# A cross-attention block on one core: its table of order and its table of places written anew

## The chip, the cores and the metric

The kernel runs on one core of a Trainium2 chip. The metric is the device time of one execution in microseconds (us). The kernel before was run three times: 654.65, 653.41 and 654.18, a median of 654.18. One more execution was taken with the hardware profiler; all durations of single instructions come from it.

## The reference

A transformer block with cross-attention in fp32: x and the context are 8 x 256 x 512 (batches, tokens, channels), 16 heads of 32 channels.

```python
residual = hidden_states
x = layer_norm(hidden_states, ln1_w, ln1_b)
q = (x @ q_w + q_b).reshape(B, LQ, H, HD).transpose(0, 2, 1, 3)
k = (encoder_hidden_states @ k_w + k_b).reshape(B, LK, H, HD).transpose(0, 2, 1, 3)
v = (encoder_hidden_states @ v_w + v_b).reshape(B, LK, H, HD).transpose(0, 2, 1, 3)
scores = jnp.einsum('bhqd,bhkd->bhqk', q, k) * scale
scores = jnp.where(mask, scores, mask_value)
attn = jax.nn.softmax(scores, axis=-1)
out = jnp.einsum('bhqk,bhkd->bhqd', attn, v).transpose(0, 2, 1, 3).reshape(B, LQ, D)
hidden = out @ cproj_w + cproj_b + residual
y = layer_norm(hidden, ln2_w, ln2_b)
y = jax.nn.gelu(y @ fc_w + fc_b, approximate=True)
return hidden + y @ proj_w + proj_b
```

fc_w is 512 x 2048, proj_w 2048 x 512.

## The kernel before, in words

**Work.** The eight batches go in two groups, 0 and 1, of four. The large products (q, k, v, the output projection o, the two of the MLP, fc and pd) are made by Strassen's method as Winograd arranged it: seven half-size products P1 to P7 in place of eight, added up in three PSUM banks X, Y and W and then evicted in pieces (t1, t2, t3, c11, c12, c21, c22; the function `quad`, L852). A tile named k1_0_W is bank W of the keys' product for group 1, half 0. An eviction that only copies is L601, one that adds a bias L606 on ScalarE and L608 on VectorE; one that adds to what is there already is L625. The sums of operands that the method needs are L623 and L625 on VectorE or GpSimd: c..t of the context, x..t and y..t of the normalized tokens, a..t of the attention, and those of the MLP's weights (fw, pw), which go to DRAM and come back as fl and pl.

**Attention.** It is done in units, named by group, quarter of the heads and batch within the group (s132: group 1, heads 12 to 15, batch 2). A unit has scores s (TensorE, four heads at once, in four PSUM banks of its own), eight evictions ev into pr (ScalarE, L614, with the mask), two maxima mx (VectorE, L1033), three copies mc (ScalarE, L1039), a fold and a transpose (VectorE, L1040 and L1042), a trip through DRAM that spreads the maximum over the partitions (md, mm), two subtractions less (VectorE L1053, or GpSimd L1057 in two pieces each), two exponentials (ScalarE, L1060), in some units halved sums ss, the product av with its row sums (TensorE, one bank), the inverse r of the sums (VectorE, L1083, L1085, L1086) and the scaling att (VectorE, L625), after which the bank of av is free. Layer norm takes BN_STATS (L802) and BN_AGGR (L804) on VectorE for each tile.

**Order.** No scheduler runs when the kernel is built. The functions only record operations, each with the engines that can do it. `Order.run` (L94) then reads two tables. PROGRAM lists all 2999 operations in one planned order; a letter behind a colon is the engine (P TensorE, V VectorE, A ScalarE, G GpSimd, S SyncE), and without a letter it is the operation's first one. Each engine gets its instructions in this order and runs them strictly in it. All DMAs are issued from SyncE's queue, in the same order. PLACES gives 1304 buffers their slot: one of eight PSUM banks for X, Y, W, s and av, or a slot in SBUF. An operation whose buffer lies in a slot that another held waits until the other's last reader is done:

```python
for word in PROGRAM.split():
    name, _, e = word.partition(":")
    o = ops.pop(name)
    o.eng = letters[e] if e else o.alts[0][0]
    order.append(o)
...
where = dict(p.split("=") for p in PLACES.split())
for o in order:
    for b in o.bufs:
        if b.slot is None and b.name in where:
            b.slot = int(where[b.name])
```

Of the kernel before, what the change touches and what calls it, by code (L numbers as in the profile page):

```python
# [127 lines left out]
rows5 c0_30:A eps_x0_1 v0_0_P2 rows4 rows6 fw0_10_0 c0t4:V v0_1_t2:V v0_0_t3:A pow_x0_1 nb_x0_1 norm_x0_11:A mk kw11
rows8 v0_1_P2 fw0_00_1 v0_0_P3 kws3:V mk~1 fw0i4_3:G fw0_10_1 cols fw0_00_0 xt0_5 v0_1_P5 fw0i4_2:V xt0_6 fw0i4_4:V
kws1:V kws2:V cols~1 k0_0_t1:A k0_1_t1:V xt0_0 k0_1_P6 v0_0_c11 xt0_7 fw0_01_0 fw0s3:V v0_1_t3:A xt0_1 fw0s1:G  # L130
fw0i5_1:G v0_1_c11 stats_x0_31 k0_0_P7 stats_x0_21 k0_1_t2:A fw0i5_2:G kw01 xt0_4 fw0_01_1 fcd0_5_False fcd0_7_False
stats_x0_00 fw0i5_3:V fw0i1_1:V fcd0_4_True fw0i7_1:G fw0i1_3:V k0_0_P6 qw00 k0_0_t2:A aggr_x0_00 fw0i7_2:V fw0i7_4:V
v0_1_P3 fw1_01_0 k0_1_P2 k0_0_P5 fw0i1_2:V fw0s2:V norm_x0_10:A aggr_x0_21 fw1_00_0 qw11 aggr_x0_31 fw0i5_4:V qw01
fw0i1_4:V k0_1_P5 vd0_0_11 stats_x0_01 aggr_x0_01 fw1_01_1 eps_x0_0 v0_1_c12:A kws4:G fw0i7_3:V v0_0_c12:A stats_x0_20
aggr_x0_20 pow_x0_0 stats_x0_30 aggr_x0_30 nb_x0_0 k0_0_t3:V k0_0_P2 fw0i2_1:G norm_x0_00:A eps_x0_2 fw1_00_1
fw0i2_2:V pow_x0_2 k0_1_P7 eps_x0_3 nb_x0_2 norm_x0_20:A fcd0_5_True norm_x0_01:V k0_1_t3:A norm_x0_21:A fcd0_7_True
cb1_11 fcd0_1_True pow_x0_3 k0_1_c11 nb_x0_3 fw0i6_3:G turn_x0_10 fw0i6_1:V fw0i6_2:G k0_0_P3 x0_10:A xt1_3 fw0i6_4:G
# [15 lines left out]
ev022_20 mx002_0 v0_1_c22 c1t1:G ev022_30 ev022_21 ev022_31 mx022_1 md020 ev022_10 less000_0:G less000_1:G v0_0_c22
cb1_20 mc002_3 ev022_01 mc002_1 mc002_2 fold002 fcd1_6_False v0_1_P4 ev022_11 mm020 q0_1_c21 v0_1_c21 mf002 ev022_00
v0_0_P4 mx022_0 exp000_0 norm_x1_11:A s010 mc022_3 mc022_1 k1_0_P1 exp000_1 cb1_33 cb1_30 cb1_32 mc022_2 ss000_0:G
cT1_20 cb1_31 v0_0_c21 ev010_30 ev010_11 md002 less020_1:V ev010_00 ev010_21 fold022 ev010_01 ev010_31 fcd1_5_True
ev010_20 ss000_1:G k1_1_P1 kd0_1_22 cT1_21 mf022 ev010_10 less020_0:V av000 s030 exp020_0 cT1_31 cT1_30 norm_x1_10:A
fcd1_6_True md022 k1_1_t1:A xt1_7 ev030_21 ev030_01 mx010_1 ev030_30 xd1_3 r000 att000 k1_0_P2 mx010_0 ev030_00
k1_0_t1:A c1t2:G k1_1_P6 exp020_1 ev030_31 ev030_20 ev030_11 k1_0_c11 mc010_1 mc010_2 mc010_3 c1t3:G kd0_1_12
ss020_0:V ev030_10 kd0_1_21 mm022 xt1_4 k1_0_P6 k1_0_t2:A ss020_1:V xt1_0 av020 stats_x1_31 mx030_1 mx030_0 aggr_x1_31  # L160
fold010 k1_1_t2:A s012 xt1_6 stats_x1_30 ev012_21 fcd1_7_True mc030_2 mc030_1 ev012_31 xt1_1 r020 k1_1_P5 stats_x1_01
att020 mf010 k1_0_P5 mm002 mc030_3 aggr_x1_30 xd1_2 kd0_0_22 k1_0_P7 less022_1:G exp022_1 md010 less022_0:G
stats_x1_00 ev012_20 exp022_0 ss022_0:V ev012_01 vd0_0_21 ku011 less002_1:V ev012_00 k1_0_t3:A mm010 less002_0:V
ev012_30 ev012_11 ev012_10 aggr_x1_01 k1_1_t3:A fold030 vd0_0_12 ss022_1:G av022 c1t4:G exp002_0 s032 vu010 xt1_5
vu030 ev032_30 ev032_11 mf030 aggr_x1_00 k1_0_c22 mx012_1 vd0_1_11 k1_1_P3 ev032_10 ev032_20 ss002_0:G mx012_0 k1_0_P3
ku001 ev032_01 ev032_31 eps_x1_3 eps_x1_0 ev032_00 less010_1:V exp002_1 k1_1_P7 ss002_1:G k1_0_P4 ev032_21 mx032_1
exp010_1 k1_0_c12:A mx032_0 vd0_0_22 stats_x1_20 av002 mc032_2 md030 mc032_3 ku021 mc032_1 k1_0_c21 r022 fold032
# [5 lines left out]
norm_x1_21:A exp030_0 mx001_0 v1_1_t1:A mc001_3 ev021_31 v1_0_t1:V v1_0_P2 v1_0_P6 att010 xd1_1 v1_1_P6 less032_0:V
xd1_7 xd1_4 ev021_20 xd1_5 v1_0_c11 mc001_2 exp030_1 s003 ss030_0:G ev021_21 mc001_1 exp032_1 ev021_30 fold001
exp032_0 mf001 mx021_0 ss032_1:V mm012 v1_0_t2:A ev003_30 v1_1_t2:V md001 ev003_01 ev003_00 ss030_1:G ev003_21 av030
ss032_0:G av032 mx021_1 mc021_3 r030 mc021_1 xb1_11 mc021_2 xb1_01 less012_0:G ev003_31 fold021 ev003_10 mf021
less012_1:V xb1_13 mm001 r032 ev003_11 ev003_20 mx003_0 ku013 exp012_0 exp012_1 v1_0_P5 v1_0_t3:A s023 md021 ev023_00
# [282 lines left out]
ps_o11=0 ot1=28 ps_o01=4 ps_o10=7  # L460
# [1053 lines left out]
```

## Time and profile before

| | |
|---|---|
| median of three runs | 654.18 us |
| the profiled execution's span, first to last instruction | 652.0 us |
| TensorE busy, share of the span | 99% |
| VectorE | 89% |
| GpSimd | 61% |
| ScalarE | 53% |
| granted clock of TensorE | 1.00 in all stages |

The span leaves out what lies ahead of the first and behind the last instruction. In the profile PE is TensorE, DVE VectorE, ACT ScalarE, POOL GpSimd, SP SyncE; L625 is line 625 of the kernel. "h<-fc_X" is a tile written from a tile read, without the numbers in the names. A group's row ends with its count, its busy time, the mean of one in ns, and the idle time ahead of it with what ended it. The attention of group 0 and the keys and values of group 1 take the time up to about 143 us, the attention of group 1 and the output projection of group 0 that up to about 288, the MLP the rest.

### The profile page before, as it was taken

The numbers are of one execution on the slowest core, as the hardware profiler recorded it, in microseconds if no ns is written. First come the engines' busy times: TensorE is split into PE (matmuls) and PEld (weight loads), VectorE is DVE, ScalarE is ACT, GpSimd is POOL, SyncE is SP. The second block draws the span as 40 slices with busy tenths as digits, with TensorE's granted clock in tenths as the row PEclk, the third lists the DMA queues.
The fourth block names the chain that finished last, engine by engine and source line by source line (L and its number), as shares of the span: only waits on it lengthen the run. The fifth ranks groups of instructions, "written<-read, shape, count | busy, mean of one in ns | idle before, by whom it ended". The sixth has DMA issues, their size and how long they took to land.

```text
span 652.0 us, 11225 instructions
## 1 busy us (share of the span) xinstructions
PE 644.3 (99%) x3793; PEld 487.7 (75%) x3793; DVE 583.2 (89%) x985; ACT 346.1 (53%) x709; POOL 395.9 (61%) x351
## 2 busy tenths in 40 slices
...
GB/s 268 306 328 324 239 251 284 226 204 152 217 224 151 130 168 232 260 267 250 257 214 250 225 272 232 293 314 170 160 222 197 215 198 204 158 190 227 173 138 97
DMA packets 206713, 144.83 MB, mean 222 GB/s; under 512 B 117136, under 2 KB 167104, under 8 KB 206656
## 3 DMA queue, kind: packets, MB, share of 16 engines
...
## 4 chain that ended last, share of the span: by engine, by line
PE 90%; DVE 4%; ACT 2%; issue 1%; DMA 1%; POOL 1%; DVEq 0%
PE pd_X L634 15%; PE fc_X L634 15%; PE fc_W L634 7%; PE pd_W L634 7%; PE av L634 6%; PE q_X L634 4%; PE v_X L634 4%; PE fc_Y L634 4%; PE k_X L634 4%; PE pd_Y L634 4%; PE s L634 4%; PE o_X L634 2%; PE v_W L634 2%; PE k_W L634 2%; PE o_W L634 2%; DVE mx L1033 2%
## 5 line engine op out<-in xcount | busy, mean ns | idle before, releaser
L614 ACT ACTIVATE pr<-s,cols 128x256 f32<-128x256 f32 x256 | 102.9, 485 | 10.7 <-PE s L634 8.2
L1057 POOL TENSOR_TENSOR pr<-pr,mm 128x512 f32<-128x512 f32 x70 | 90.2, 1318 | 7.2 <-DMA xt<-in_x_dram 5.0
L1237 ACT ACTIVATE h<-h,cols 128x256 f32<-128x256 f32 x128 | 55.2, 499 | 61.2 <-DVE h L625 45.2
L1033 DVE TRANSPOSE_TENSOR_REDUCE mx<-pr 128x32 f32<-128x1024 f32 x64 | 76.9, 1216 | 1.5 <-ACT pr L614 1.3
L1060 ACT ACTIVATE pr<-pr 128x1024 f32<-128x1024 f32 x64 | 66.5, 1061 | 12.1 <-POOL pr L1057 9.0
L625 DVE TENSOR_TENSOR h<-fc_X,h 128x512 f32<-128x512 f32 x80 | 52.4, 675 | 5.5 <-PE fc_X L634 4.7
L625 POOL TENSOR_TENSOR ss<-pr 128x512 f32<-128x512 f32 x24 | 31.5, 1325 | 14.2 <-ACT pr L1060 11.8
L625 DVE TENSOR_TENSOR h<-fc_W,h 128x512 f32<-128x512 f32 x48 | 32.0, 677 | 5.0 <-PE fc_W L634 4.4
L1053 DVE TENSOR_TENSOR pr<-pr,mm 128x1024 f32<-128x1024 f32 x29 | 35.2, 1229 | 0.0
L1039 ACT COPY mx<-mx 32x64 f32<-32x64 f32 x96 | 23.2, 243 | 15.9 <-DVE mx L1033 14.7
L623 POOL TENSOR_TENSOR z1t<-h,z1t 128x512 f32<-128x512 f32 x6 | 8.0, 1360 | 26.1 <-PE pd_Y L634 12.3
L625 POOL TENSOR_TENSOR tq<-tq,rq 128x512 f32<-128x512 f32 x8 | 10.1, 1272 | 21.7 <-DMA rq<-hd 15.4
L634 PE MATMUL pd_X<-z0i,pl 128*128 128x256 f32 x96 | 22.5, 379 | 0.0
L634 PE MATMUL fc_W<-y1i,fl 128*128 128x256 f32 x84 | 20.7, 379 | 0.0
L625 DVE TENSOR_TENSOR h<-fc_Y,h 128x512 f32<-128x512 f32 x24 | 15.9, 672 | 5.3 <-PE fc_Y L634 5.3
L634 PE MATMUL pd_W<-z1i,pl 128*128 128x256 f32 x88 | 20.6, 379 | 0.0
L1040 DVE TENSOR_REDUCE mx<-mx 32x32 f32<-32x256 f32 x32 | 18.4, 578 | 2.2 <-ACT mx L1039 2.0
L634 PEld LDWEIGHTS pd_X<-z0i,pl 128*128 128x128 f32 x96 | 18.2, 190 | 2.5
L811 POOL TENSOR_TENSOR rs_y<-rs_y,neg_half 128x2 f32<-128x2 f32 x8 | 10.2, 1289 | 15.3 <-DMA pl<-prd 7.7
L634 PE MATMUL pd_X<-h,pl 128*128 128x256 f32 x80 | 18.9, 379 | 0.0
L601 ACT COPY h<-fc_X 128x512 f32<-128x512 f32 x16 | 9.0, 594 | 18.5 <-PE fc_X L634 15.6
L625 DVE TENSOR_TENSOR po<-pd_X,po 128x256 f32<-128x256 f32 x24 | 9.9, 414 | 9.6 <-PE pd_X L634 9.4
...
## 6 DMA issues: line engine op xcount, KB each, us to landing
...
```

The costliest lines, as they stand in the source:

```text
L601: (nc.scalar.copy if e == "ACT" else nc.vector.tensor_copy)(to(), of_())
L614: lambda e: nc.scalar.activation(to(), of_(), AF.Identity, bias=bias(), scale=1.0))
L625: E[e].tensor_tensor(to(), in0(), in1(), op)
L634: nc.tensor.matmul(o(), l(), r(), start=first, stop=True, skip_group_check=True)
L811: lambda e, rs=rs: nc.gpsimd.tensor_tensor(tile_of(rs)[:, 2:4], tile_of(rs)[:, 0:2], neg_half[:, 0:2], ALU.pow), lock=True)
L1033: T.op(f"mx{u}_{h}", [("DVE", 1.126)], [(pr[h], None)], [(mx, [h])], lambda e, h=h: nc.vector.tensor_reduce(tile_of(mx)[:, 0:64].rearrange ...
L1039: lambda e, a=a: nc.scalar.copy(tile_of(mx)[0:32, 64 * a : 64 + 64 * a], tile_of(mx)[32 * a : 32 * a + 32, 0:64]))
L1040: T.op(f"fold{u}", [("DVE", 0.38)], [(mx, [0, 1, 2, 3, 4])], [(mx, [5])], lambda e: nc.vector.tensor_reduce(tile_of(mx)[0:32, 256:288], ti ...
L1053: nc.vector.tensor_tensor(p_, p_, m_[:, None, :].to_broadcast([P, 2, 512]), ALU.subtract)
L1057: E[e].tensor_tensor(p_, p_, m_, ALU.subtract)
L1060: lambda e, h=h: nc.scalar.activation(tile_of(pr[h]), tile_of(pr[h]), AF.Exp), table="exp")
L1237: lambda e, f=f, b=b, c=c: nc.scalar.activation(at(h[f][b], c), at(h[f][b], c), AF.Gelu_apprx_tanh, bias=col(c_fcb + f * 4 + c), scale=1.0 ...
```

## The change

Only the two tables change; not a line of code does. Both have the same 2999 words and the same 1304 buffers. 153 words change their engine: 64 from VectorE to GpSimd, 48 from GpSimd to VectorE, 23 from ScalarE to VectorE, 18 from VectorE to ScalarE. 972 buffers change their slot. On TensorE most operations stay within four positions of where they stood; the largest moves are in the second MLP product of group 1.

One line of PROGRAM before and the one that holds the same eviction after, and lines of PLACES:

```diff
-mx013_1 mx013_0 q1_1_t1:A av003 mx031_0 q1_0_t1:A x1_30:A r001 ev033_11 ev033_21 mc013_3 mc013_2 mc031_2 q1_0_P6
+mc031_2 mc031_1 q1_1_t1:V r003 q1_0_P6 pw0_00_01 hid0_2 vu013 pw0_00_11 q1_0_t2:V fold031 att003 mf031 mc013_3 mc013_2
-mm010=4 ss010=4 av020=3 r020=1 rc020=4 att0_10=88 vu030=10 s030_0=3 s030_1=5 s030_2=6 s030_3=4 pr030_0=8 pr030_1=10
+mm010=4 ss010=70 av020=5 r020=5 rc020=9 att0_10=88 vu030=1 s030_0=5 s030_1=4 s030_2=0 s030_3=6 pr030_0=8 pr030_1=10
-rc122=1 att1_11=48 s132_0=1 s132_1=0 s132_2=5 s132_3=7 pr132_0=4 pr132_1=66 mx132=2 mm132=80 av110=1 r110=3 rc110=3
+mx112=0 mm112=54 av122=7 r122=1 rc122=6 att1_11=48 s132_0=7 s132_1=5 s132_2=3 s132_3=0 pr132_0=66 pr132_1=4 mx132=1
```

Bank 3, that of k1_0_W in both tables, is held by av020 ahead of it before, and by av000, one unit earlier, after (`av000=0` has become `av000=3`). Bank 7 is that of o0_0_W in both; the scores' buffer that holds it last is s132_3 before and s132_0 after.

The first place is on VectorE, in the attention of group 0. Before, att0_10 (the scaling of unit 020) stands behind the statistics (BN_STATS) of tiles x1_3 and x1_0:

```order
L802 BN_STATS st_x1_3_1092<-k1_1_11_1025 128x6
L1033 TENSOR_REDUCE mx030_1094<-pr030_1_1028 128x2x16
L1033 TENSOR_REDUCE mx030_1094<-pr030_0_1030 128x2x16
L804 BN_AGGR mv_x1_3_1097<-st_x1_3_1092 128x2
L1040 TENSOR_REDUCE mx010_1032<-mx010_1032 32x32
L802 BN_STATS st_x1_3_1092<-xt1_0_1077 128x6
L1083 TENSOR_REDUCE rc020_1122<-av020_1079 128x8
L1085 RECIPROCAL rc020_1122<-rc020_1122 128x8
L1086 STREAM_TRANSPOSE r020_1125<-rc020_1122 128x256
L802 BN_STATS st_x1_0_1129<-vw11_255 128x6
L625 TENSOR_TENSOR att0_10_1131<-av020_1079,r020_1125 128x256
L1042 STREAM_TRANSPOSE mx010_1032<-mx010_1032 32x32
```

After, in the same place (att0_00 and att0_10 are the scalings of units 000 and 020):

```order
L802 BN_STATS st_x1_0_1086<-xt1_0_1029 128x6
L1033 TENSOR_REDUCE mx030_1065<-pr030_1_1049 128x2x16
L625 TENSOR_TENSOR att0_00_1100<-av000_971,r000_1022 128x256
L1083 TENSOR_REDUCE rc020_1102<-av020_1071 128x8
L1085 RECIPROCAL rc020_1102<-rc020_1102 128x8
L1086 STREAM_TRANSPOSE r020_1105<-rc020_1102 128x256
L1040 TENSOR_REDUCE mx010_1037<-mx010_1037 32x32
L802 BN_STATS st_x1_0_1086<-xt1_0_1029 128x6
L804 BN_AGGR mv_x1_3_1144<-st_x1_3_1002 128x2
L1042 STREAM_TRANSPOSE mx010_1037<-mx010_1037 32x32
L802 BN_STATS st_x1_3_1002<-k1_1_11_1045 128x6
L625 TENSOR_TENSOR att0_10_1149<-av020_1071,r020_1105 128x256
```

The scaling that frees bank 3 for k1_0_W is att0_10 before, next to last here, and att0_00 after, third here; of the three BN_STATS that stood ahead of it one still does.

The second place is the first evictions of q for group 1. Before, they are on ScalarE (the two L606), between scalings of x and evictions of scores:

```order
L766 ACTIVATE x1_10_1825<-x1_10_1825,cols_87 128x512
L606 ACTIVATE v0_1_11_271<-q1_1_X_1811,cols_87 128x512
L606 ACTIVATE q1_0_11_1894<-q1_0_X_1839,cols_87 128x512
L766 ACTIVATE x1_10_1825<-x1_10_1825,cols_87 128x512
L614 ACTIVATE pr033_0_1902<-s033_1_1855,cols_87 128x256
L614 ACTIVATE pr033_1_1904<-s033_2_1857,cols_87 128x256
L1039 COPY mx013_1872<-mx013_1872 32x64 x2
```

After, they stand on VectorE (the two L608), among the maxima and the inverses:

```order
L1033 TENSOR_REDUCE mx013_1886<-pr013_1_1807 128x2x16
L608 TENSOR_SCALAR kws4_362<-q1_1_X_1852,cols_87 128x512
L1083 TENSOR_REDUCE rc003_1913<-av003_1889 128x8
L1085 RECIPROCAL rc003_1913<-rc003_1913 128x8
L1086 STREAM_TRANSPOSE r003_1916<-rc003_1913 128x256
L608 TENSOR_SCALAR xt0_6_431<-q1_0_X_1849,cols_87 128x512
L1040 TENSOR_REDUCE mx031_1774<-mx031_1774 32x32
```

In this stretch the same eviction moved from ScalarE to VectorE four times.

The third place is on ScalarE, at the scores of unit 132, whose banks the output projection takes next. Before, bank 7 holds s132_3, and its evictions stand behind copies of mx112:

```order
L614 ACTIVATE pr132_1_2488<-s132_2_2480,cols_87 128x256
L1039 COPY mx112_2490<-mx112_2490 32x64 x2
L614 ACTIVATE pr132_1_2488<-s132_2_2480,cols_87 128x256
L614 ACTIVATE pr132_0_2506<-s132_1_2478,cols_87 128x256
L1039 COPY mx112_2490<-mx112_2490 32x64
L614 ACTIVATE pr132_0_2506<-s132_1_2478,cols_87 128x256
L614 ACTIVATE pr132_1_2488<-s132_3_2482,cols_87 128x256 x2
```

After, both evictions of s132_0, in bank 7, stand first, and all copies of mx112 come later:

```order
L614 ACTIVATE pr132_0_2492<-s132_0_2468,cols_87 128x256 x2
L614 ACTIVATE pr132_0_2492<-s132_1_2470,cols_87 128x256
L614 ACTIVATE pr132_1_2496<-s132_2_2472,cols_87 128x256
L614 ACTIVATE pr132_1_2496<-s132_3_2474,cols_87 128x256
L614 ACTIVATE pr132_0_2492<-s132_1_2470,cols_87 128x256
L614 ACTIVATE pr132_1_2496<-s132_2_2472,cols_87 128x256
L1039 COPY mx112_2460<-mx112_2460 32x64
L614 ACTIVATE pr132_1_2496<-s132_3_2474,cols_87 128x256
```

What moved is which scores' buffer lies in the projection's bank, and that the copies no longer stand ahead of its evictions.

More of the change, by code (lines that the diff above doesn't have):

```diff
@@ L128 @@
[L128 to L137, printed above, removed]
@@ L153 @@
[L153 to L162, printed above, removed]
@@ L163 @@
[L163 to L167, printed above, removed]
@@ L173 @@
[L173 to L177, printed above, removed]
@@ L208 @@
-less122_1:G s132 ev132_20 mx112_0 mx112_1 mc112_1 o0_1_P5 md130 r100 mc112_3 ev132_21 ev132_10 mc112_2 md110 o0_1_P7
-ev132_11 ev132_30 ev132_31 o0_0_c12 exp102_0 o0_1_t3 ev132_01 fold112 pw0_10_11 exp122_1 o0_0_P7 att100 mf112 mm130
-ev132_00 md112 o0_1_P2 mx132_1 o0_1_c22 o0_0_c22 mx132_0 mm110 mc132_3 stats_y0_21 o0_1_c11 stats_y0_20 o0_1_P4 mm112
-pw0_01_11 mc132_1 o0_1_c21 exp102_1 exp122_0 aggr_y0_20 less120_0:G o0_0_P4 exp120_0 stats_y0_10 stats_y0_11 o0_0_c21
-less120_1:G aggr_y0_11 less130_1:G mc132_2 less130_0:G pw0_01_00 less110_1:G aggr_y0_21 aggr_y0_10 pw0_11_01 exp130_1
@@ new lines @@
+rows3 kw10 kw11 rows0 vws1:V vws2:V rows5 k0_0_P1 k0_1_P1 kws3:G turn_c0_20 turn_c0_30 v0_1_P6 v0_0_P6 v0_1_t2:A
+c0_30:A vw01 xt0_5 rows6 rows8 rows7 fw0_11_0 vws3:G c0t3:V c0_20:V vws4:V fw0i4_1:V c0t4:V v0_1_P5 v0_0_P2 kws1:G
+kws2:G kw01 kws4:G rows4 rows1 xt0_2 mk fw0_00_1 rows2 fw0i4_3:V fw0i4_2:V v0_0_c11 k0_0_P7 stats_x0_10 k0_1_P2 mk~1
+stats_x0_21 fw0_00_0 fw0_10_1 xt0_7 xt0_1 xt0_3 aggr_x0_10 cols cols~1 stats_x0_01 stats_x0_31 v0_1_P2 stats_x0_11
+aggr_x0_11 fw0_10_0 k0_1_t1:A k0_1_P6 fw0i1_3:V aggr_x0_01 v0_0_t2:A fw0s3:V fw0s1:V fw0s2:V qw00 fw0_01_1 xt0_6
@@ new lines @@
+k1_1_P1 v0_1_c21 less020_1:V k1_0_P1 av000 fold022 ev010_10 cT1_21 ev010_20 ev010_00 mf022 ev010_21 exp020_1 ev010_11
+less020_0:V cb1_31 cb1_33 cT1_31 xt1_7 cT1_30 stats_x1_31 md002 fcd1_5_True ev010_01 s030 r000 fcd1_6_True md022 ku003
+vd0_0_22 xt1_0 mm022 k1_0_t1:A ev010_30 ev010_31 mx010_1 mx010_0 k1_0_P2 k1_0_c11 exp020_0 k1_1_t1:A ev030_00 ev030_30
+ev030_31 ev030_10 norm_x1_11:A ev030_11 ev030_01 ev030_21 norm_x1_10:A ev030_20 ss020_0:V ss020_1:V c1t2:G mx030_0
+k1_0_P6 k1_1_P6 av020 xt1_6 fcd1_7_True stats_x1_00 c1t3:G less022_1:G mc010_2 k1_0_t2:A k1_1_t2:A xt1_1 mc010_1
@@ new lines @@
+mc010_3 mx030_1 att000 r020 mm002 vd0_0_21 xd1_3 ku021 kd0_1_12 s012 fold010 exp022_1 ev012_20 ev012_01 ev012_10
+k1_1_P5 k1_0_P5 k1_0_P7 less022_0:G exp022_0 stats_x1_01 aggr_x1_31 mf010 stats_x1_30 md010 att020 aggr_x1_01
+aggr_x1_30 kd0_1_22 vd0_1_11 ku031 ss022_1:G ev012_00 ev012_11 ev012_21 ev012_30 aggr_x1_00 mc030_2 ev012_31 ss022_0:V
+k1_1_t3:A mc030_3 k1_0_t3:A mc030_1 less002_1:V eps_x1_3 less002_0:V mx012_0 fold030 k1_0_c22 exp002_0 av022 s032
+mf030 mx012_1 ev032_31 ev032_21 ev032_01 exp002_1 ev032_20 ev032_30 mm010 less010_1:V eps_x1_0 xt1_4 vd0_0_12 kd0_0_22
@@ new lines @@
+ev001_01 ev021_10 nb_x1_3 ev021_11 ev021_01 ev001_00 less030_1:G norm_x1_30:A norm_x1_21:V less030_0:V norm_x1_31:V
+norm_x1_20:A v1_0_P1 k1_1_P4 v1_1_P1 exp030_1 exp030_0 mx001_0 att010 v1_0_P2 v1_0_t1:V v1_0_P6 v1_1_t1:V mc001_3
+mc001_1 ev021_30 ev021_31 v1_1_P6 md032 vu012 vu030 ku013 mm032 less032_0:V k1_1_c21 mx021_0 less032_1:G xd1_1 xd1_0
+s003 exp032_1 mc001_2 fold001 mf001 ss032_1:V exp032_0 ev021_21 ev021_20 ss030_0:G ss030_1:G v1_0_c11 v1_1_t2:V
+mx021_1 v1_0_t2:A xd1_5 md012 xd1_6 xd1_4 ev003_30 xd1_7 av030 mm012 r030 att030 ss032_0:G v1_0_P5 ev003_00 xb1_12
@@ new lines @@
+av100 mc110_3 mc110_2 mx130_0 ev112_20 ev112_11 o0_0_t3 o0_0_P3 a0t4:V ev112_21 mm120 r100 ev112_01 mc130_2 ev112_00
+ev112_10 mx112_0 mc130_3 mc130_1 ev112_30 mc110_1 ev112_31 fold130 s132 fold110 mf130 md130 pw0_11_00 o0_1_P5 mx112_1
+mf110 md110 ev132_00 ev132_01 ev132_10 ev132_20 ev132_30 ev132_11 ev132_21 mc112_3 ev132_31 less122_0:G less122_1:G
+mc112_1 exp122_0 mc112_2 exp102_1 o0_0_c12 o0_1_t3 mx132_0 mx132_1 att100 o0_1_P2 less120_0:G o0_1_P7 o0_1_c22
+less120_1:G o0_0_P7 mm130 fold112 o0_1_c11 o0_0_c22 mf112 o0_1_P4 o0_0_P4 less130_0:G less130_1:G mm110 pw0_10_00 s101
@@ new lines @@
+mc103_1 ev123_20 fc012_P1 fc012_t1 fc012_P2 fold103 pw0i5_3:G pw0s4:G y0i6_1:G pw0i5_1:G fc012_c11 mf103 y0i6_2:G
+fc006_P6 fc006_t2 fc016_P6 fc016_t2 fc006_P2 fc006_c11 pw0i5_2:G y0i6_4:G y0i2_1:G pw0i5_4:G y0i2_2:G pw0i3_1:G
+y0i2_4:G y0i2_3:G pw0i3_3:G ev123_01 fc012_P6 s111 ev111_10 ev111_00 ev111_30 ev111_01 ev111_11 mm121 mx123_0 fc002_t1
+fc012_t2 fc016_P5 mx123_1 fc002_P6 md103 prd0_5_True fl016_3 prd0_3_False fc016_t3 fc002_t2 ev111_21 mc123_2 mc123_1
+mc123_3 mx111_0 ev111_20 less121_1:G less121_0:G pw0i3_2:G y0i6_3:G ev111_31 pw0i3_4:G pw0i4_3:G mm103 less103_1:G
@@ L364 @@
-v0_1_12=19 s000_0=2 s000_1=0 s000_2=5 s000_3=7 pr000_0=10 pr000_1=24 mx000=1 mm000=34 ss000=74 s020_0=2 s020_1=0
-s020_2=7 s020_3=4 pr020_0=44 pr020_1=26 mx020=2 mm020=46 ss020=56 s002_0=6 s002_1=0 s002_2=7 s002_3=3 pr002_0=66
-pr002_1=38 mx002=1 mm002=56 ss002=76 s022_0=3 s022_1=1 s022_2=2 s022_3=0 pr022_0=58 pr022_1=68 mx022=0 mm022=4
-ss022=24 av000=0 r000=10 rc000=1 att0_00=78 vu010=3 s010_0=0 s010_1=6 s010_2=3 s010_3=4 pr010_0=80 pr010_1=22 mx010=2
-mm010=4 ss010=4 av020=3 r020=1 rc020=4 att0_10=88 vu030=10 s030_0=3 s030_1=5 s030_2=6 s030_3=4 pr030_0=8 pr030_1=10
@@ L369 @@
-mx030=0 mm030=70 ss030=80 av002=2 r002=12 rc002=1 att0_01=58 vu012=1 s012_0=0 s012_1=7 s012_2=4 s012_3=6 pr012_0=26
-pr012_1=44 mx012=2 mm012=50 ss012=68 av022=5 r022=11 rc022=8 att0_11=38 vu032=7 s032_0=7 s032_1=6 s032_2=4 s032_3=0
-pr032_0=56 pr032_1=68 mx032=1 mm032=80 ss032=46 av010=5 r010=2 rc010=8 ku001=6 s001_0=4 s001_1=6 s001_2=7 s001_3=3
-pr001_0=76 pr001_1=66 mx001=1 mm001=28 ss001=46 av030=7 r030=12 rc030=0 ku021=2 s021_0=3 s021_1=4 s021_2=6 s021_3=7
-pr021_0=4 pr021_1=72 mx021=0 mm021=46 ss021=48 av012=0 r012=6 rc012=5 ku003=5 s003_0=0 s003_1=5 s003_2=4 s003_3=3
@@ L459 @@
[L459 to L460 removed]
+cq0_00=36 cq0_10=88 cq0_01=26 cq0_11=76 ps_cols=6 ps_c0_00_0=1 c0_00=22 ps_c0_00_1=2 ps_c0_10_0=6 ps_c0_10_1=3
+ps_c0_20=6 c0_10=82 ps_c0_30=0 ps_c0_01=6 c0_01=34 ps_c0_11=1 ps_c0_21=7 c0_11=54 ps_c0_31=0 xt0_0=10 xt0_1=3 xt0_2=20
+xt0_3=24 xt0_4=56 xt0_5=2 xt0_6=18 xt0_7=72 st_x0_0=9 mv_x0_0=4 rs_x0_0=2 xn_x0_00=11 xn_x0_01=53 st_x0_1=5 mv_x0_1=8
@@ new lines @@
+pr002_1=38 mx002=1 mm002=56 ss002=58 s022_0=5 s022_1=4 s022_2=3 s022_3=7 pr022_0=68 pr022_1=58 mx022=0 mm022=4
+ss022=24 av000=3 r000=9 rc000=4 att0_00=78 vu010=7 s010_0=5 s010_1=4 s010_2=0 s010_3=7 pr010_0=22 pr010_1=80 mx010=1
+mm010=4 ss010=70 av020=5 r020=5 rc020=9 att0_10=88 vu030=1 s030_0=5 s030_1=4 s030_2=0 s030_3=6 pr030_0=8 pr030_1=10
+mx030=2 mm030=4 ss030=80 av002=6 r002=3 rc002=0 att0_01=58 vu012=10 s012_0=7 s012_1=0 s012_2=4 s012_3=6 pr012_0=44
+pr012_1=26 mx012=1 mm012=50 ss012=4 av022=5 r022=3 rc022=0 att0_11=38 vu032=11 s032_0=4 s032_1=7 s032_2=6 s032_3=0
@@ new lines @@
+pr032_0=56 pr032_1=68 mx032=0 mm032=80 ss032=4 av010=7 r010=4 rc010=9 ku001=1 s001_0=4 s001_1=2 s001_2=7 s001_3=3
+pr001_0=66 pr001_1=76 mx001=2 mm001=46 ss001=46 av030=5 r030=3 rc030=9 ku021=0 s021_0=2 s021_1=3 s021_2=5 s021_3=6
+pr021_0=14 pr021_1=72 mx021=0 mm021=80 ss021=6 av012=7 r012=13 rc012=4 ku003=6 s003_0=4 s003_1=7 s003_2=0 s003_3=6
+pr003_0=30 pr003_1=70 mx003=2 mm003=4 av032=3 r032=8 rc032=7 ku023=8 s023_0=0 s023_1=5 s023_2=4 s023_3=7 pr023_0=8
+pr023_1=10 mx023=0 mm023=46 av001=7 r001=8 rc001=9 ku011=7 vu011=5 s011_0=6 s011_1=5 s011_2=3 s011_3=0 pr011_0=82
```

577 lines of the change are left out of this document (290 added, 287 removed).

## The prediction

> **What bounds the kernel now.** I read the page first: its span, its busy times and its chain.
>
> ```profile
> span 652.0 us, 11225 instructions
> PE 644.3 (99%) x3793; PEld 487.7 (75%) x3793; DVE 583.2 (89%) x985; ACT 346.1 (53%) x709; POOL 395.9 (61%) x351
> PE 90%; DVE 4%; ACT 2%; issue 1%; DMA 1%; POOL 1%; DVEq 0%
> ```
>
> TensorE is busy for 99% of the span and carries 90% of the chain that ended last. The program's matmuls are the same after the change, so what can be won is TensorE's idle time, and what can be lost is new idle time. The profiled execution's span of 652.0 us stands 2.2 below the median of the three runs (654.18); every sum below is made against 652.0, and 2.2 is added at the end. What a measurement of this kernel can tell from no change is 0.2%, 1.3 us.
>
> Next come the busy times by stage, cut where the work changes. The columns are the stretch, its length, and the busy time and count of each engine.
>
> ```profile
> 60.00:112.00 52.00, 50.50 (x267) 25.85 (x266) 48.64 (x84) 38.70 (x90) 31.36 (x29) 1.00 0.92 261
> 143.00:288.00 145.00, 143.60 (x1212) 96.19 (x1204) 140.52 (x252) 133.14 (x280) 126.91 (x102) 1.00 0.69 200
> 370.00:652.00 282.00, 278.50 (x1317) 243.39 (x1315) 238.00 (x380) 70.00 (x150) 121.02 (x103) 1.00 0.79 205
> ```
>
> From 143 to 288, the attention of the second group, TensorE has 145.00 - 143.60 = 1.4 us idle and VectorE 145.00 - 140.52 = 4.5: two engines are near their limit there, and what is added to VectorE beyond 4.5 must lengthen the stage. After 370 VectorE has 44 us to spare, and the granted clock is 1.00 throughout.
>
> The waits of TensorE, summed by releaser, show the idle time that can go (us in total, times, longest):
>
> ```profile
> PE k_W L634 <- DVE mx L1042: 1.5, 1, 1.5
> PE o_W L634 <- ACT pr L614: 1.0, 1, 1.0
> PE av L634 <- ACT pr L614: 0.3, 1, 0.3
> ```
>
> The timeline around the first (start, length, engine, operation; in brackets the wait):
>
> ```profile
> 99.49 0.92 SPq L588 DMA_DIRECT2D xt<-in_x_dram  x2
> 107.84 0.70 DVE L802 BATCH_NORM_STATS2 st_x<-xt 128x6 f32<-128x512 f32 x1 [2.08 <-DMA xt<-in_x_dram]
> 110.36 0.41 DVE L625 TENSOR_TENSOR att<-av,r 128x256 f32<-128x256 f32 x1
> 110.91 1.95 PE L634 MATMUL k_W<-c1t,xt 128*128 128x512 f32 x4 [1.50 <-DVE mx L1042]
> ```
>
> and around the second:
>
> ```profile
> 226.93 12.19 POOL L1057 TENSOR_TENSOR pr<-pr,mm 128x512 f32<-128x512 f32 x9 [1.05 <-DMA mm<-md]
> 227.12 2.24 DVE L625 TENSOR_TENSOR a0t<-att,a0t 128x1024 f32<-128x1024 f32 x1
> 232.40 0.50 ACT L1039 COPY mx<-mx 32x64 f32<-32x64 f32 x2 [1.19 <-DVE mx L1033]
> 234.02 1.20 ACT L614 ACTIVATE pr<-s,cols 128x256 f32<-128x256 f32 x3
> 235.28 1.99 PE L634 MATMUL o_W<-xt,a0t 128*128 128x256 f32 x8 [1.01 <-ACT pr L614]
> ```
>
> The first is k1_0_W, held up because its PSUM bank, 3, still held av020. That bank comes free with the scaling of att020 at 110.36, and this stood on VectorE behind a BN_STATS that waited 2.08 us for a tile of x. The page names the transpose at L1042 as releaser; I take it to be the scaling just ahead, since nothing of that transpose goes to k1_0_W. The second is o0_0_W in bank 7, held by the last evictions of s132, which stood on ScalarE behind mc112 copies that waited 1.19 for VectorE.
>
> **The change, part by part.** *The stall of k1_0_W.* In the new places bank 3 holds av000 ahead of k1_0_W, one unit earlier; its scaling, att0_00, stands on VectorE ahead of the one for av020, att0_10, as the rows of the change show. Between the two lie two BN_STATS, an aggregation, the three inverse instructions, a fold and its transpose: 2 x 0.70 by the row at 107.84, 0.58 and 0.18 by rows quoted below, so 2.2 us with the inverse not yet counted, more than the 1.5 waited. I take the whole 1.5 as gained. Bounds: 1.5, since no more was waited, and 0.5 if the tile of x reaches the BN_STATS just ahead of att0_00 another 1.7 us later than before (2.2 - 1.5 + 1.0). What is late next is av020, whose bank, 5, goes to av022 next and to no product of the keys.
>
> *The stall of o0_0_W.* Bank 7 now holds s132_0, evicted first, ahead of the mc112 copies, and o0_0_P7 stands behind two more products. The stall goes. But it lies in the stage where VectorE had only 4.5 us to spare, so I give it no gain of its own: it is part of the stage's sum, next.
>
> *The stage from 143 to 288.* Between the same two operations (the inverse after av030, the eviction ahead of s111) the order holds 250 VectorE instructions before, 259 after; ScalarE goes from 279 to 272. The prices:
>
> ```profile
> L1033 DVE TRANSPOSE_TENSOR_REDUCE mx<-pr 128x32 f32<-128x1024 f32 x64 | 76.9, 1216 | 1.5 <-ACT pr L614 1.3
> L1040 DVE TENSOR_REDUCE mx<-mx 32x32 f32<-32x256 f32 x32 | 18.4, 578 | 2.2 <-ACT mx L1039 2.0
> L625 DVE TENSOR_TENSOR h<-fc_X,h 128x512 f32<-128x512 f32 x80 | 52.4, 675 | 5.5 <-PE fc_X L634 4.7
> L608 DVE TENSOR_SCALAR kws<-k_X,cols x1: 751/751/751, 27.4 to 27.4; 128x512 f32<-128x512 f32 x1
> L601 DVE COPY vw<-v_X 128x512 f32<-128x512 f32 x4 | 2.7, 666 | 0.0
> L768 DVE TENSOR_SCALAR y<-y,cols 128x512 f32<-128x512 f32 x4 | 2.2, 538 | 0.0
> 99.01 0.42 DVE L625 TENSOR_TENSOR att<-av,r 128x256 f32<-128x256 f32 x1
> 99.35 1.24 DVE L1033 TRANSPOSE_TENSOR_REDUCE mx<-pr 128x32 f32<-128x1024 f32 x1
> L1042 DVE STREAM_TRANSPOSE mx<-mx 32x32 f32<-32x32 f32 x17 | 2.9, 178 | 0.1
> ```
>
> Added: four L608 (4 x 0.751 = 3.00), two L601 (2 x 0.666 = 1.33), two PSUM additions (2 x 0.675 = 1.35), one L768 (0.54), one fold with its transpose (0.578 + 0.178 = 0.76). Removed: one L1033 (1.22) and one addition of 256 columns (0.41, as the one at 99.01 took). Sum 5.35. Neighbours overlap: the instruction at 99.35 starts 0.34 after one that took 0.42, so 0.08 each for nine, 0.7 less: **+4.6** of VectorE work. By itself that eats all 4.5 of idle time. What pays for it are VectorE's own waits there:
>
> ```profile
> DVE mx L1033 <- ACT pr L614: 1.3, 1, 1.3
> DVE h L625 <- PE fc_W L634: 0.6, 1, 0.6
> DVE mx L1040 <- ACT mx L1039: 0.5, 1, 0.5
> ```
>
> ScalarE gives up seven instructions, the added L608 among them, so I take its two waits, 1.3 + 0.5 = 1.8, as gone; bounds none and all three, 2.4. And there are instructions that took longer than their form:
>
> ```profile
> L625 DVE TENSOR_TENSOR pw0s<-pw,pw 128x1024 f32<-128x1024 f32 x2 | 2.4, 1215 | 0.0
> L625 DVE TENSOR_TENSOR a0t<-att,a0t 128x1024 f32<-128x1024 f32 x1 | 2.2, 2243 | 0.0
> L625 DVE TENSOR_TENSOR pw0i<-pw 128x256 f32<-128x256 f32 x1 | 1.5, 1493 | 0.0
> L625 DVE TENSOR_TENSOR pw0i<-pw0i,pw 128x256 f32<-128x256 f32 x1 | 1.3, 1332 | 0.0
> L625 DVE TENSOR_TENSOR pw0i<-pw0s 128x256 f32<-128x256 f32 x3 | 1.1, 406 | 0.0
> ```
>
> a0t took 2.243 against 1.215 for the same shape, two pw0i sums 1.493 and 1.332 against 0.406: 1.03 + 1.09 + 0.93 = 3.05 lost. Each has two operands in SBUF, and while a0t ran, at 227.12, GpSimd was in its row of nine subtractions: the two take turns at a port. The new order puts other pairs side by side, so of the 3.05 I take half as gone, 1.5; bounds none and all. The stage: +4.6 - 1.8 - 1.5 = **+1.3**.
>
> The Trainium skill ("SBUF — State Buffer", "SBUF: two separate sides") says that this port pair is locked for a whole instruction and the loser blocks. The three losses (0.93 to 1.09, under one 1.35 GpSimd instruction, 12.19 / 9) agree. By that rule alone any order meets the lock as often, nothing of 3.05 would go, and the sum would be 655.5.
>
> *TensorE's own work.* Counted in the order, it comes back to full tiling after scores or values 37 times, before 34. The chain shows a return's price:
>
> ```profile
> 79.54 1.08 PE s L634 x16
> 80.62 1.93 PE v_W L634 x8
> 85.54 1.72 PE q_W L634 x4
> ```
>
> Eight v_W matmuls right after scores took 1.93, a product without scores ahead of it 1.72: 0.2 each, 0.6 for three. Two or three lie in the stage above, where TensorE waits for VectorE: no cost while that cover holds, 0.6 without it. *The rest*: VectorE's words move between stages (-7.6 us after 545, +1.5 from 380 to 470, where by the third row of the stages it has 44 to spare), two table loads of ScalarE go, SP's 606 issues stay: nothing.
>
> Sum: 652.0 - 1.5 + 1.3 = 651.8, and with 2.2: **654.0**.
>
> **The rivals.**
>
> A, slower: VectorE becomes the bound. It keeps its waits and its port losses, and the stage grows by the full 4.6: 652.0 - 1.5 + 4.6 = 655.1, so 657.3; with the 0.6 of TensorE's returns 657.9. It decides once what VectorE saves of waits falls short of about 3. For it: evictions moved from ScalarE (133.14 of 145.00 busy) to the fuller engine. Against it: VectorE's idle time names ScalarE twice. The Trainium skill ("Perfetto Trace Analysis", "Optimizing Scalar/DVE Operations") has the rule behind it: with a saturated DVE, hand work to Scalar, and between GPSIMD and DVE a move might not help. Here work goes the other way.
>
> B, faster: all three waits (2.4) and all the port losses (3.05) go: 4.6 - 5.45 = -0.8, so 652.0 - 1.5 - 0.8 = 649.7, 651.9 in all; with the 1.0 and 0.3 of TensorE's other waits on top, 650.6. For it: both TensorE stalls have their bank exchanged for one that is free earlier, and ScalarE has more room. Against it: VectorE would have to run 140 us with hardly a gap.
>
> C, the change doesn't do what it says at k1_0_W: the load of x is late for the BN_STATS ahead of att0_00 by 2.2 us more, TensorE waits as long, and only the +1.3 is left: 653.3, 655.5 in all. Against it: of the three BN_STATS only one still stands ahead of the scaling.
>
> **How the numbers follow.** The forecast gets 0.45, A 0.20, B 0.29, C 0.06. The forecast's own range, from the port losses' 1.5 to either side and the 1.0 of the first stall, is 652.4 to 656.5; of its 0.45 I put 0.11 at faster by over 0.2%, 0.25 within and 0.09 slower. C is split evenly, being 0.2% off. So faster 0.11 + 0.29 = 0.40, the same 0.25 + 0.03 = 0.28, slower 0.09 + 0.03 + 0.20 = 0.32. The range is B's lowest to A's highest, 650.6 to 657.9.
>
> **What would show it.** Right: no wait at k_W near 110; the stage's elapsed time between the same two operations longer by about 1.3, VectorE idle in it under 3, stretched sums there half as long. For A: VectorE idle still over 4, or stretched sums of 3 us again, and TensorE waiting for VectorE in that stage. For B: that stage no longer than before. The forecast is wrong if the difference comes from before 60 or after 370, where I expect none.

## The result and the profile after

The changed kernel took 662.97 us (median of four runs) against 653.79 for the kernel before (four runs): ratio 1.0119, with a 95% interval of 1.0083 to 1.0155. It is slower by about 8 us, above the range of the prediction. The first profile of it is of an execution of 671.23 us in which one instruction waited unusually long (last section); the readings here are of a second profile, of an execution of 662.57 us, its span of 660.8 beside the 652.0 of before.

The head of its page:

```profile
span 660.8 us, 11224 instructions
PE 647.7 (98%) x3793; PEld 487.4 (74%) x3793; DVE 596.9 (90%) x974; ACT 340.1 (51%) x702; POOL 422.0 (64%) x368
```

VectorE has 11 instructions fewer than before (974, 985) and is busy 13.7 us longer (596.9, 583.2). The instructions themselves have become longer. The stages, first of before (those that the prediction left out), then of the changed kernel (stretch, length, busy time and count of PE, PEld, DVE, ACT, POOL, then clock, DMA share and GB/s):

```profile
0.00:60.00 60.00, 59.02 (x246) 39.13 (x247) 46.96 (x83) 21.58 (x33) 26.97 (x35) 1.00 0.94 309
112.00:143.00 31.00, 30.91 (x239) 17.86 (x241) 29.16 (x56) 29.87 (x62) 23.39 (x19) 1.00 0.72 219
```

```profile
0.00:60.00 60.00, 57.56 (x243) 38.10 (x244) 47.44 (x83) 21.05 (x33) 26.84 (x34) 1.00 0.94 302
60.00:112.00 52.00, 51.53 (x269) 26.12 (x268) 49.83 (x73) 36.63 (x85) 34.90 (x33) 1.00 0.89 263
112.00:143.00 31.00, 28.66 (x184) 16.28 (x183) 30.51 (x58) 27.55 (x57) 22.40 (x18) 1.00 0.71 223
143.00:288.00 145.00, 143.60 (x1240) 94.32 (x1240) 142.62 (x257) 131.19 (x275) 124.78 (x100) 1.00 0.65 190
370.00:652.00 282.00, 279.89 (x1308) 243.84 (x1308) 241.65 (x364) 73.80 (x158) 141.51 (x117) 1.00 0.80 206
```

The stage of the prediction's long sum, 143 to 288, holds as much TensorE time as before, 143.60 of 145. New idle time stands in stages to which the prediction gave nothing: 2.4 us up to 60 (before 1.0) and 2.3 from 112 to 143 (before 0.1). These stages are cut by the clock and hold somewhat different work in the two kernels. The same two operations, the inverse after av030 and the scores s111, stand here, first before, then in the changed kernel:

```profile
142.97 0.40 DVE L1083 TRANSPOSE_TENSOR_REDUCE rc<-av 128x8 f32<-128x256 f32 x1
288.11 1.15 PE L634 MATMUL s<-v,k 32*128 32x256 f32 x16
```

```profile
147.60 0.40 DVE L1083 TRANSPOSE_TENSOR_REDUCE rc<-av 128x8 f32<-128x256 f32 x1
293.14 1.15 PE L634 MATMUL s<-kws,k 32*128 32x256 f32 x16
```

Of the 8.8 us between the two spans, 4.6 are lost ahead of this stage, 0.4 in it (145.5 against 145.1) and 3.8 behind it. Seen from TensorE, 5.4 of the 8.8 are more idle time (13.1 against 7.7) and 3.4 are longer matmuls in sum (647.7 against 644.3, both x3793); why these became longer, the profile doesn't show. The waits of TensorE in the changed kernel:

```profile
PE o_X L634 <- DVE hid L625: 1.9, 1, 1.9
PE k_Y L634 <- DVE v L625: 1.0, 1, 1.0
PE fc_Y L634 <- DVE kw L625: 0.9, 1, 0.9
PE av L634 <- DVE att L625: 0.8, 1, 0.8
PE av L634 <- DVE ss L625: 0.8, 1, 0.8
PE k_W L634 <- DVE mx L1042: 0.8, 1, 0.8
PE q_W L634 <- DVE q L625: 0.5, 1, 0.5
```

Nearly every one is for VectorE, small, and they are spread over the program. Why VectorE is late shows in the timeline ahead of the one at k_Y (start, length, engine, operation):

```profile
19.10 1.71 POOL L625 TENSOR_TENSOR vw<-kw,kw 128x512 f32<-128x512 f32 x1
19.61 1.49 DVE L625 TENSOR_TENSOR fw0i<-fw 128x256 f32<-128x256 f32 x1
20.89 1.33 POOL L625 TENSOR_TENSOR kws<-vw,kw 128x512 f32<-128x512 f32 x1
21.02 2.28 DVE L625 TENSOR_TENSOR c0t<-c,c0t 128x1024 f32<-128x1024 f32 x1
22.30 2.13 POOL L625 TENSOR_TENSOR kws<-kw,kws 128x512 f32<-128x512 f32 x1
23.23 1.48 DVE L625 TENSOR_TENSOR fw0i<-fw 128x256 f32<-128x256 f32 x1
24.64 0.94 DVE L625 TENSOR_TENSOR fw0i<-fw0i,fw 128x256 f32<-128x256 f32 x1
25.50 0.68 DVE L625 TENSOR_TENSOR v<-v_Y,v 128x512 f32<-128x512 f32 x1
26.23 1.13 PE L634 MATMUL k_Y<-c,kw 128*128 128x512 f32 x2 [0.96 <-DVE v L625]
```

The sum at 19.61 needs 0.41 us by itself and took 1.49; it ends at 21.10, 0.29 us after GpSimd's sum of 19.10 (20.81). The next pairs read the same: 23.30 is 1.08 after 22.22, and 24.71 is 0.28 after 24.43. Each VectorE sum lasts as long as what GpSimd had left to do and, 0.13 less, its own time. So three sums that the prediction would have priced at 0.41 + 1.22 + 0.41 took 5.25, a fourth, at 24.64, took 0.94, the addition at 25.50 came late, and TensorE waited 0.96.

Groups of VectorE, before and after, show the same at other places (mean of one in ns after the comma):

```profile
L625 DVE TENSOR_TENSOR fw0i<-fw 128x256 f32<-128x256 f32 x3 | 1.6, 552 | 0.0
L808 DVE TENSOR_SCALAR rs_x<-mv_x 128x2 f32<-128x2 f32 x8 | 1.1, 153 | 0.1
L1428 DVE TENSOR_TENSOR hid<-hid,cb 128x1024 f32<-128x1024 f32 x2 | 2.4, 1218 | 0.0
```

```profile
L625 DVE TENSOR_TENSOR fw0i<-fw 128x256 f32<-128x256 f32 x5 | 4.3, 861 | 0.0
L808 DVE TENSOR_SCALAR rs_x<-mv_x 128x2 f32<-128x2 f32 x8 | 5.0, 630 | 0.1
L1428 DVE TENSOR_TENSOR hid<-hid,cb 128x1024 f32<-128x1024 f32 x2 | 5.7, 2856 | 0.0
```

An instruction on two columns, L808, went from 153 ns to 630 on the mean. Added up over all VectorE instructions with SBUF operands, the time above their form's own is about 17 us before and 35 after.

### The profile page after: what moved, and what is told of

It is laid out like the page before. It is cut to its first block, busy times and chain, and to the rows that moved or that the text cites. A ratio compares the mean times of both kernels' runs of the same rounds, so it can differ in the third digit from the quotient of the medians.

```text
span 669.5 us, 11224 instructions
## 1 busy us (share of the span) xinstructions
PE 649.9 (97%) x3793; PEld 487.5 (73%) x3793; DVE 600.4 (90%) x974; ACT 340.4 (51%) x702; POOL 419.5 (63%) x368
## 5 line engine op out<-in xcount | busy, mean ns | idle before, releaser
L614 ACT ACTIVATE pr<-s,cols 128x256 f32<-128x256 f32 x256 | 102.2, 482 | 15.9 <-PE s L634 13.1
L625 POOL TENSOR_TENSOR ss<-pr 128x512 f32<-128x512 f32 x24 | 34.2, 1438 | 11.7 <-ACT pr L1060 8.1
L1053 DVE TENSOR_TENSOR pr<-pr,mm 128x1024 f32<-128x1024 f32 x29 | 37.8, 1321 | 2.5 <-DMA mm<-md 2.5
L625 POOL TENSOR_TENSOR tq<-tq,rq 128x512 f32<-128x512 f32 x9 | 12.8, 1428 | 20.4 <-DMA rq<-hd 8.8
L623 POOL TENSOR_TENSOR z0i<-h,z0i 128x512 f32<-128x512 f32 x6 | 9.4, 1582 | 16.8 <-DMA kw<-in_L_xattn_proj_w_dram 9.6
L1428 POOL TENSOR_TENSOR hid<-hid,cb 128x1024 f32<-128x1024 f32 x6 | 17.2, 2862 | 4.2 <-DMA hid<-in_x_dram 2.2
L634 PE MATMUL fc_W<-y1i,fl 128*128 128x256 f32 x76 | 19.2, 380 | 0.0
L634 PE MATMUL pd_X<-z1i,pl 128*128 128x256 f32 x80 | 18.9, 379 | 0.0
L623 POOL TENSOR_TENSOR z1i<-z1t,z1t 128x512 f32<-128x512 f32 x4 | 5.8, 1477 | 19.6 <-DVE z1i L625 19.6
L634 PE MATMUL av<-pr,ones 128*32 128x256 f32 x256 | 17.1, 383 | 0.9 <-DVE att L625 0.8
L634 PE MATMUL fc_X<-y,fl 128*128 128x256 f32 x68 | 17.2, 383 | 0.6 <-DVE att L625 0.6
```

Of the source, the lines that this page charges most:

```text
L614: lambda e: nc.scalar.activation(to(), of_(), AF.Identity, bias=bias(), scale=1.0))
L623: nc.gpsimd.tensor_tensor(to()[:, ts(k, 512)], in0()[:, ts(k, 512)], in1()[:, ts(k, 512)], op)
L625: E[e].tensor_tensor(to(), in0(), in1(), op)
L634: nc.tensor.matmul(o(), l(), r(), start=first, stop=True, skip_group_check=True)
L1053: nc.vector.tensor_tensor(p_, p_, m_[:, None, :].to_broadcast([P, 2, 512]), ALU.subtract)
L1428: lambda e, v=v: E[e].tensor_tensor(v(), v(), cb.t[:, None, :].to_broadcast([P, 2, D]), ALU.add), lock=True)
```

## The experiments

Theory P: VectorE and GpSimd wait for each other at a port, and the new tables make them meet twice as often. Theory V: VectorE is over-full because of the evictions that ScalarE handed over (the first expectations call it theory 1). Theory O: the new order and places make TensorE wait, whatever the engines do (there theory 3). Theory 2 of these puts the loss on one addition, a0t4.

**The changed kernel again**, unaltered.

> The changed kernel once more, with a second profile. Theory 1 (VectorE is over-full from 60 to 290 us: the evictions that ScalarE handed over make it late, and TensorE waits for it): 660 to 664 us, and in the new profile the same waits of TensorE for VectorE, above all between 100 and 290, with the addition of a0t4 not necessarily stretched. Theory 2 (one addition, a0t4, that stood 6.27 us on VectorE beside a row of GpSimd subtractions, makes the loss): in a run of 660 us a0t4 takes 2.3 us or less, in one of 664 or more about 6. Theory 3 (the new order of words and the new places, whatever the engines, make TensorE wait): 660 to 664, waits spread over engines and DMAs.

663.16 us, ratio 1.0126 (1.0067 to 1.0186). TensorE's waits are those above. a0t4 took 1.26 us there, and the loss was all the same: theory 2 doesn't explain it.

**Old engines in the new order, and the reverse.** The letters of the 153 words exchanged, for instance

```diff
-q1_1_t1:V
+q1_1_t1:A
```

> The new order and the new places, but all 153 words that changed their engine on their old engine again. Theory 1: most of the loss goes, 654 to 657 us. Theory 2: a0t4 stays on VectorE in the same place, so 660 to 664. Theory 3: 660 to 664.

> The old order and the old places, with the 153 words on their new engines. Theory 1: slower than before by most of the loss, 658 to 663 us. Theory 2: 653 to 656. Theory 3: 653 to 656. None of them accounts for words that were put on an engine where the old order has no room for them: that would make it slower still.

700.60 us (ratio 1.0676, 1.0636 to 1.0716) and 692.90 us (1.0540, 1.0477 to 1.0604). Both are far slower than either kernel; no theory gave the first, and of the second the expectation had only the direction. Order and engines of a table belong together, and exchanging all of one for the other tells nothing about what either costs. The two are inconclusive.

**a0t4 on GpSimd.**

```diff
-a0t4:V
+a0t4:G
```

> The changed kernel with one word altered: a0t4 on GpSimd in place of VectorE, ahead of the subtractions of unit 122 there. Theory 1: VectorE is relieved by 1.2 us, GpSimd takes 2.6: 659 to 663 us. Theory 2: 655 to 658, TensorE's wait of 4.1 us at o_W gone. Theory 3: 659 to 663.

663.25 us, ratio 1.0102 (1.0060 to 1.0144): no change against the changed kernel, and theory 2 falls.

**GpSimd without its reads, in both kernels.** In place of each sum of 256 columns and more, GpSimd did this:

```diff
-E[e].tensor_tensor(to, a, b, op)
+nc.gpsimd.tensor_tensor(to[..., :8], a[..., :8], b[..., :8], op)
+for _ in range({256: 1, 512: 2, 1024: 2}[n]):
+    nc.gpsimd.memset(to[..., 8:], 1.0)
```

> The kernel before, in which every GpSimd sum or subtraction of 256 columns and more does only its first 8 columns and then fills the rest with a constant, once or twice, so that GpSimd reads almost nothing; the result is not the block's any more. Instructions, order and waits of all other engines stay. Theory P (VectorE and GpSimd wait for each other at a port, and the new tables make them meet twice as often: instructions of VectorE that stood longer than their form lost about 17 us in all before and 35 after): here VectorE's stretched instructions all but vanish, and the kernel gains 1 to 4 us, 650 to 653. Theory O (the new order and places make TensorE wait whatever the port does) and theory V (VectorE has too much work): the same gain, as it is the other kernel of this pair that tells them apart.

> The changed kernel with the same alteration of GpSimd's sums. Theory P: the gap of 8 to 9 us between the two kernels closes, this one stands within 2 us of the other of the pair, 650 to 654. Theory O: a gap of 6 us or more stays. Theory V: a gap of 3 to 6 stays, since VectorE keeps the evictions that ScalarE handed over.

650.17 us for the altered kernel before (ratio to the kernel before 0.9940, 0.9919 to 0.9961) and 651.85 for the altered changed one (0.9961, 0.9946 to 0.9977). A gap of 1.2% has become one of 0.2%, which the two intervals don't tell from none. Their busy times, the kernel before first:

```profile
PE 642.7 (99%) x3793; PEld 486.8 (75%) x3793; DVE 567.3 (88%) x985; ACT 345.8 (53%) x709; POOL 330.8 (51%) x890
```

```profile
PE 643.6 (99%) x3793; PEld 487.1 (75%) x3793; DVE 564.1 (87%) x974; ACT 339.4 (52%) x702; POOL 347.6 (53%) x929
```

VectorE runs the same instructions as in the unaltered kernels in 567.3 us in place of 583.2, and in 564.1 in place of 596.9. So the meeting cost VectorE 15.9 us before and 32.8 after, while its own work is 3.2 us less in the new tables. And GpSimd was not just made short; a replaced subtraction of 512 columns takes one of each of these, the fill twice (kernel before):

```profile
L1519 POOL MEMSET pr<- 128x504 f32 x140 | 72.4, 517 | 4.0
L1517 POOL TENSOR_TENSOR pr<-pr,mm 128x8 f32<-128x8 f32 x70 | 17.3, 247 | 10.0 <-DMA mm<-md 5.7 <-DVE mx L1042 3.2 <-DVE h L625 1.2
```

0.247 + 2 x 0.517 = 1.28 us, where a subtraction that met nothing took 1.27. Sums of 256 columns did become shorter: 0.20 for the 8 columns and 0.30 for one fill, in place of 0.73. And GpSimd doesn't stop waiting: its own instructions were stretched by 28 us before and 40 after, and the sums of 8 columns, 0.20 each by itself, still are, by 18 and 24. So a part of the gain may be GpSimd's, and the test doesn't separate the two. It does speak against the plain amount of GpSimd's work as the cause: GpSimd is still busy 16.8 us longer in the altered changed kernel (347.6 against 330.8), and the gap is closed all the same. TensorE's waits point to VectorE's delay: those for VectorE at o_X and k_Y, listed above, are gone there, and that at fc_Y is down from 0.9 to 0.2. Theory P holds for 6 to 7 of the 8 us; 1.4 to 1.7 us of the gap stay, no more than the runs scatter, and these may be order and places.

**Ten words back on ScalarE**, all of those between 130 and 205 us that had gone to VectorE: v1_1_t1, v1_0_t3, v1_1_t3, q1_1_t1, q1_0_t2, q1_0_c12, q1_1_t3, norm_x1_21, norm_x1_31 and x1_00.

```diff
-q1_1_t1:V
-q1_0_t2:V
+q1_1_t1:A
+q1_0_t2:A
```

> The changed kernel with the ten words of the attention stages that went from ScalarE to VectorE on ScalarE again (evictions of v and q for group 1, two normalizations, one scaling of x). Theory V: 656 to 659. Theory P: these evictions read PSUM and meet no port, so within 1.5 us of the changed kernel, 661 to 664. Theory O: 661 to 664 too.

662.17 us, ratio 1.0103 (1.0079 to 1.0127), within the interval of the changed kernel. VectorE's busy time fell by 5.4 us:

```profile
PE 646.9 (98%) x3793; PEld 488.0 (74%) x3793; DVE 591.5 (90%) x964; ACT 344.9 (52%) x712; POOL 420.6 (64%) x368
```

and nearly nothing of it reached the end. Theory V falls as far as these ten go; the other 13 words that went from ScalarE to VectorE, ahead of 80 us and in the MLP, were not tried. (Of the two L608 of q shown with the change, the first is the eviction q1_1_t1 of the rows of before; the second is q1_0_t2, which moved too, while q1_0_t1 stayed on ScalarE.)

**The first stall by itself**, in the kernel before.

```diff
-k1_0_W=3 av022=5
+k1_0_W=5 av022=3
```

> The kernel before with two places exchanged: k1_0_W in bank 5, free long before it, and av022 in bank 3, so that k1_0_W no longer waits for the scaling of unit 020. It measures the first stall by itself. If the stall's 1.5 us lie on the path: 1.0 to 1.5 us faster than before. If something else is late next there (VectorE's additions into the same product): within 0.5 us of before.

654.62 us, ratio 0.9991 (0.9972 to 1.0010). The matmul that had waited 1.50 starts at 109.27, without a wait, and the next scaling holds up the next scores:

```profile
109.27 1.88 PE L634 MATMUL k_W<-c1t,xt 128*128 128x512 f32 x4
123.02 0.40 DVE L625 TENSOR_TENSOR att<-av,r 128x256 f32<-128x256 f32 x1
123.47 1.13 PE L634 MATMUL s<-qws,ku 32*128 32x256 f32 x10 [0.67 <-DVE att L625]
```

**Where the meetings hurt.** GpSimd's reads taken out as above, but only in the first 360 words of the changed kernel, or only from word 1880 on.

> The changed kernel with GpSimd's sums cut to 8 columns and a fill only in the first 360 of the 2999 words, up to about 80 us, where it sums weights for the MLP; the result is not the block's any more. Theory P (the port) says that the loss arises where the two engines meet: TensorE lost about 2.5 us more than before by 80 us, so 1.5 to 2.5 us faster than the changed kernel, 660 to 661.5, and the waits behind 100 us stay. Theory O: within 1 us of the changed kernel.

> The same only from word 1880 on, about 365 us, the MLP. Theory P: the addition into hid and the MLP's sums no longer meet; TensorE lost 3 to 4 us more than before behind 360 us, so 2 to 4 us faster than the changed kernel, 658 to 661. Theory O: within 1 us of it.

658.48 us (ratio 1.0072, 1.0044 to 1.0099) and 659.84 (1.0084, 1.0064 to 1.0104), so about 4.5 and 3 us less than the 662.97 of the changed kernel by the medians, 3 and 2.3 by the ratios, whose intervals overlap with the changed kernel's (1.0083 to 1.0155). The first did better than expected: counted in the traces, TensorE had lost 2.8 us less than in the changed kernel after its first 100 us of work, and 3.7 less after 240, so what was on time early lost less later. Both expectations gave these gains to theory P, and theory O at most 1 us. Both ends of the program seem to carry a share. The stage that the prediction watched was not tried by itself; in the changed kernel's second profile it lost 0.4 us, but in that of the second of these two, where its words are unaltered, it took 147.2 (146.22 to 293.38) in place of 145.5, so it varies by more than that between executions.

**Toward a faster kernel.** Three banks exchanged in the kernel before, and then also two stretched sums moved to GpSimd, behind a0t3:

```diff
-k1_0_W=3 av022=5 s001_3=3
+k1_0_W=5 av022=3 s001_3=5
```

```diff
-pw0i1_2:V ... pw0i1_3:V ... a0t3:G
+a0t3:G pw0i1_2:G pw0i1_3:G
```

> The kernel before with three places exchanged: k1_0_W in bank 5, av022 in 3 and s001_3 in 5, so that neither k1_0_W nor the scores of unit 001 wait for a scaling. If the stall is worth its length: 1.0 to 1.5 us faster than before. If VectorE and ScalarE, not the bank, set the pace there: within 0.7.

> The same, and two sums of pw0i1 that stood 1.33 and 1.49 us on VectorE beside GpSimd (0.41 where nothing meets them) on GpSimd, behind a0t3. Theory P: VectorE gains 2.8 us in the stage where it is tight, GpSimd takes 1.5: another 0.5 to 1.5 us faster, 651 to 653. If GpSimd is late instead for the subtractions behind them: no gain.

The first took 655.16 us, ratio 1.0005 (0.9988 to 1.0021). The second took 652.81 to 655.06 in five of its eleven executions, ratio 0.9989 (0.9963 to 1.0015) by these alone, and 662.94 to 666.90 in the other six; the one of the six that was profiled has the long wait of the last section. In the first kernel, with all three banks, neither k_W nor the scores wait any more, and TensorE waits elsewhere instead:

```profile
PE av L634 <- POOL ss L625: 0.6, 1, 0.6
PE v_X L634 <- DVE vw L601: 0.4, 1, 0.4
```

No version that beats the kernel before came of it.

## Why the prediction was wrong

The step that failed is the last one of the part by part, "*The rest*: ... nothing", together with the place where port losses were counted. I read them in one stage, 143 to 288, because TensorE was near VectorE's pace there, found 3.05 us and took half as gone. In that stage they did shrink (a0t4 took 1.26 in place of 2.24). But 112 words had changed between just the two engines that share the port, most of them ahead of 80 us and behind 370, and there I counted instructions at their undisturbed price and saw 44 us to spare. The time that VectorE lost in meetings with GpSimd went from 15.9 to 32.8 us, and TensorE, which has to wait for VectorE's additions to its products all through the program, lost 6 to 7 us with it. The prediction's remark that any order meets the lock as often did not hold either: one order lost twice as much as the other.

Point by point:
- *k1_0_W's stall gone*: right as far as the bank goes. In the changed kernel's second profile the eight k_X matmuls ahead of it run straight into k1_0_W:

```profile
108.19 3.70 PE L634 MATMUL k_X<-c1t,vw 128*128 128x512 f32 x8
111.72 1.88 PE L634 MATMUL k_W<-c1t,kws 128*128 128x512 f32 x4
```

  But its worth was put too high: 1.5, bounds 0.5 and 1.5. Alone it measured 0.9991 (0.9972 to 1.0010), with the next bank freed as well 1.0005 (0.9988 to 1.0021); the second leaves out a gain of 1.5 us, and neither leaves out 0.5. By the traces, what TensorE no longer waited at one bank it waited at the next places. In the changed kernel 0.8 each at av and at another k_W stand in its place.
- *The stage from 143 to 288, +1.3*: the outcome was better than the sum: 0.4 us between the same two operations, in one profile. VectorE is idle 145.00 - 142.62 = 2.4 us in it (I wrote under 3), TensorE's 143.60 is unchanged. VectorE's waits for ScalarE there are gone.
- *Evictions from ScalarE to VectorE*, the heart of rival A: ten of the 23, undone alone, changed nothing. A was the right sign by the wrong mechanism. The Trainium skill's rule that I put behind it ("Perfetto Trace Analysis", "Optimizing Scalar/DVE Operations") has two halves, and the one I passed over, that moves between GPSIMD and DVE might not help since they share a port, is the one that bears on the result; here the kernel even became slower.
- *0.6 us for TensorE's returns*: no run tells it apart.
- *The test that I set*, wrong if the difference comes from before 60 or after 370: it came from there, and from 112 to 143; by the same two operations, 4.6 us from ahead of the stage and 3.8 from behind it.

What stays open: which of the moved words make the meetings (engine or position), since neither table can be had with the other's letters; how much of the loss is GpSimd's own delay; and the last 1.4 to 1.7 us between the two kernels without reads.
